# A 3x3 grouped convolution whose images are prepared ahead: parts made one image further ahead, from image 15 on

## The chip, the cores and the metric

The kernel runs on one core of one Trainium2 chip. The metric is the device time of one execution in microseconds (us); the figure given is the median of several runs.

## The reference

The input `x` is 160 images of 128 channels and 32 x 32 pixels in fp32. They are normalised, convolved with weights that are first brought onto a coarse grid, and added to the input:

```python
def _gn(v, G=32, eps=1e-5):            # groups of 4 channels, each image by itself
    g = v.reshape(B_, G, C_ // G, H_, W_)
    m = jnp.mean(g, axis=(2, 3, 4), keepdims=True)
    s = jnp.var(g, axis=(2, 3, 4), keepdims=True)
    return ((g - m) / jnp.sqrt(s + eps)).reshape(v.shape)

# weights: U is (5, 128*128*9); two levels of flooring over the range of U
s1 = (max(U) - min(U)) / 3;  v1 = s1 * floor(U / s1)
s2 = s1 / 5;                 v2 = s2 * floor((U - v1) / s2)
w = (v1 + v2).reshape(640, 128, 3, 3)

# image i uses weight set i % 5 (five groups of a grouped convolution), 3x3, padding 1
x = x + conv(_gn(x), w)
```

## The kernel before, in words

**Order of the images.** The kernel takes the images set by set: 32 images with the first weight set, then 32 with the second, and so on; "image i" below is a place in that order. A chunk is two images, 1 MB, loaded by one DMA. `xpool` holds `CHUNKS` of them.

**The arithmetic.** TensorE multiplies fp16 numbers, so a normalised image is split into a high and a low fp16 part and both are convolved. Output rows are made in pairs, an even and an odd one, from combinations of input rows (or, for a "combined" image, of input columns) and of weights, which takes fewer matmuls than nine taps for each. There are two kinds of image. A *direct* one (`combined(i)` false) gives `hi` (ScalarE, L645) and a low part: `lo` (VectorE, L748) and its row combinations `rows` (L761, L769, L770). A *combined* one gives `v` in fp32, made by GpSimd (L675, L705) and VectorE (`combine`: L687, L694), then `vh` on ScalarE (L735) and `vl` on VectorE (L741). Up to image 29 combined and direct images alternate; up to 129 three of five are combined; from 130 on three of four.

**TensorE's part.** `conv(i)` first runs `sums_of_pairs(i + 1)`: the sums and differences that both output rows of image i + 1 share, into two PSUM tiles `m2` and `m1` (`m1a`, `m1b`), which need `vl` or `rows` of image i + 1. Then `main(i)` adds the rest to the two banks `eo` of image i. Between the two, ScalarE copies `m2` out (`leave`, L888), and VectorE makes the start of both banks from `m1` and that copy (`pairs`, L900 for the even one and L902 for the odd one). When `conv(i)` is over, ScalarE copies the banks out (L926), and GpSimd issues a DMA that adds them to the output in HBM (L950), where the input has been stored from the chunk before (L965). The first three and the last four images are added by hand on VectorE instead (`by_hand`).

**Step i of the loop in `run`.** One step is one image on TensorE. The program is written in the order in which each engine's queue shall run it; nothing is reordered later. In step i (from image 3 on), before the change:

- VectorE: the low part or `vl` of image i + 2; one or two small instructions of the next weight set (`later.take`); `pairs(i + 1)`; the scales of a finished statistics group; `combine(i + 4)`.
- ScalarE: the first statistics pass of the images due (L241), the copy-out of image i - 1, `leave(i + 1)`, `hi` or `vh` of image i + 3, the second statistics pass (L248).
- GpSimd: the power of a statistics group (L286, then `scales_by_vector` with L307 and L309 on VectorE), then its part of `v` or of z for image i + 4 (L675 and L705, or L711). `beside_pairs` makes these wait for the last VectorE instruction but one of the low part, so that they run while VectorE is busy with PSUM in `pairs`. GpSimd and its DMA issue follow in the same queue.
- SP: loads a chunk when the images `CHUNKS` places before it have been read (`consumed`), and stores a chunk four steps after its load.

**Statistics.** Images are measured in groups of 2, 4 or 8, by ScalarE, eight of them by VectorE (`BY_VECTOR`); `ahead` says up to which image in step i. A group's numbers take three more steps over TensorE (L256, L273), `deviations_by_vector` (L296 to L302), ScalarE and GpSimd. `shift` (L309) is used only by `normalise`, on ScalarE, for the first image of a group when that is a direct one.

Of the kernel before, what the change touches and what calls it, by code (L numbers as in the profile page):

```python
# [11 lines left out]
ALU = mybir.AluOpType  # L12
# [9 lines left out]
NB = 2  # L22
# [14 lines left out]
class Later:  # L37


    def __init__(self, steps=(), pace=0.0):  # L40
        self.steps = iter(steps)
        self.pace, self.due = pace, 0.0
        self.scalar = False
# [131 lines left out]
def last_of(steps, last=None):  # L175
    for last in steps:
        pass
    return last
# [27 lines left out]
class Statistics:  # L206
# [5 lines left out]
    def __init__(self, nc, small, gavg, mhalf, nb, scale, name):  # L212
        self.nc, self.small, self.gavg, self.mhalf = nc, small, gavg, mhalf
        self.nb, self.scale, self.name = nb, scale, name
        self.late = False

        self.mv = self.tile("mv", [nb, 2])

# [85 lines left out]
    def scales_by_vector(self):  # L304

        vector = self.nc.vector
        vector.tensor_scalar_mul(self.rstd, self.rstd, self.scale)  # L307
        self.shift = self.tile("shift", [self.nb])
        vector.tensor_tensor(self.shift, self.ngm, self.rstd, ALU.mult)  # L309

    def scales(self):
        nc = self.nc
# [72 lines left out]
class Main:  # L385
# [21 lines left out]

    STAT_LEAD = 14  # L410
    LOAD_LEAD = 18
    CHUNKS = 12
    STEADY = 7
    BY_VECTOR = (8, 10, 11, 14, 19, 24, 29, 34)
    FIFTHS = 30
# [10 lines left out]
    def __init__(self, tc, ctx, keep, x, u, out):  # L426
        self.tc = tc
        nc = self.nc = tc.nc
        self.imgs, C, self.H, self.W = x.shape
        P = self.P = nc.NUM_PARTITIONS  # L430
        assert C == P and self.H * self.W == 1024
        self.per_set = self.imgs // N_SETS
        self.xv = x.rearrange("(b n) c h w -> n c b (h w)", n=N_SETS)
        self.ov = out.rearrange("(b n) c h w -> n c b (h w)", n=N_SETS)
        self.uv = u.rearrange("n (o i k) -> n o i k", o=C, k=TAPS)

        def pool(name, bufs, **kw):
            return ctx.enter_context(tc.tile_pool(name=name, bufs=bufs, **kw))

        self.const = pool("const", 1)  # L440
        self.qpool = pool("quant", 1)
        self.wpool = pool("weights", 2)
        self.upool = pool("u", 1)
        self.xpool = pool("x", self.CHUNKS)
        self.zpool = pool("z", 2)
        self.parts = pool("parts", 4)
        self.rows = pool("rows", 4)
        self.wide = pool("wide", 2)
        self.wide_parts = pool("wide_parts", 3)
        self.evac = pool("evac", 2)  # L450
        self.sums = pool("sums", 3)
        self.unread = pool("unread", 1)
        self.small = pool("small", 3)
        self.ps_eo = pool("ps_eo", 2, space=PSUM)
        ps_m = pool("ps_m", 1, space=PSUM)
        ps_small = pool("ps_small", 1, space=PSUM)
        self.steps = Steps(nc, keep)

        self.m1a, self.m1b, self.m2_ps = (
            ps_m.tile([P, self.H // 2, self.W], F32, tag=name, name=name)  # L460
            for name in ("m1a", "m1b", "m2")
        )
        self.pair = [self.m1a, self.m2_ps]

        small = ps_small.tile([P, 512], F32, tag="small", name="small")
        self.pt, self.pg = small[:, : ROW * P].rearrange("p (k o) -> p k o", k=ROW), small[:, ROW * P :]
        self.chunks, self.z, self.hi, self.v, self.eo, self.m2 = {}, {}, {}, {}, {}, {}
        self.sum, self.stored = {}, {}
        self.tables, self.wts, self.across = {}, {}, {}
        self.columns = []  # L470

        cuts = [0, 2, 4, 8, 12, 16, 20, *range(24, self.imgs + 1, 8)]
        self.groups = [range(a, b) for a, b in zip(cuts, cuts[1:])]
        self.group_of = {i: k for k, g in enumerate(self.groups) for i in g}
        self.stats = {}
# [131 lines left out]
    def stats_of(self, k):  # L607
        if k not in self.stats:
            self.stats[k] = Statistics(
                self.nc, self.small, self.gavg, self.mhalf, len(self.groups[k]),  # L610
                self.steps.lift, k,
            )
            self.stats[k].late = self.groups[k].start not in self.HURRIED
        return self.stats[k]

    def measure(self, i, stages=(0, 1)):
# [343 lines left out]
    def store_input(self, c):  # L960
# [6 lines left out]
            return  # L967
        self.stored.update((i, self.store(i)) for i in images)

    def consumed(self, c):  # L970

        return max(i + 2 if self.by_hand(i) else i - 2 for i in range(c * NB, c * NB + NB))

    def run(self):
        nc, P = self.nc, self.P
# [53 lines left out]
        def measure(stage, *images):  # L1029
            for i in images:  # L1030
                self.measure(i, (stage,))
# [73 lines left out]
        later, turned = Later(), []  # L1105
        for i in range(self.imgs):
# [30 lines left out]
            else:  # L1137
                j = i - 1
                self.conv(i, on_the_way)
            ahead = i + min(10 + i // 4, self.STAT_LEAD + 1)  # L1140
            to_measure = range(measured, min(self.imgs, ahead))
            measured += len(to_measure)
            if i == 2:
# [3 lines left out]
            if n + 1 < N_SETS:  # L1147
                if b == (4 if n == 0 else 1):
                    later = Later(
                        (s for col in self.COLS for s in self.make_column(n + 1, col, "later")),  # L1150
                        36 / (self.per_set - 6 - b),
                    )
# [4 lines left out]
            if i < self.FIRST:  # L1157

                if i == 0:
                    measure(0, 8, 9, 10)  # L1160
                if i == 1:
                    self.normalise(4)
                    self.high_part(4)
                if i == 2:
                    self.leave(3)
                    self.normalise(5)
                    measure(1, 9)
                    self.high_part(5)
                    self.pairs(3)
                    self.low_part(4)  # L1170
                    run(self.combinations(4))
                    measure(0, 11)
                self.residual(j)
            else:

                last = None
                if self.combined(i + 2):
                    last = last_of(self.low_combined(i + 2))
                elif i + 2 < self.imgs:
                    self.low_part(i + 2)  # L1180
                    later.take(1)
                    last = last_of(self.combinations(i + 2))
                last = later.take(2 if self.combined(i + 2) else 1, last)
                if i + 4 < self.imgs:
                    before = self.last_but_one(last)
                    for st in scaled:
                        self.after(st.power(), before)
                    self.beside_pairs(i + 4, before)
                if i > self.FIRST and self.by_hand(j):
                    self.residual(j)  # L1190
                for k in by_scalar:
                    self.measure(k, (0,))
                if i > self.FIRST and not self.by_hand(j):
                    self.residual(j)
                    self.accumulate(j)
                part = i + 3 < self.imgs and not self.combined(i + 3)
                if i + 1 < self.imgs:
                    self.leave(i + 1)
                for st in ready:
                    if not st.late:  # L1200
                        st.deviations()
                if part:
                    if self.by_scalar_too(i + 3):
                        self.normalise(i + 3)
                    self.high_part(i + 3)
                if self.combined(i + 3):
                    self.high_combined(i + 3)
                for k in by_scalar:
                    self.measure(k, (1,))
            for st in middle:  # L1210
# [7 lines left out]
            for n_of, col in turned:  # L1218
                self.keep_taps(n_of, col)
                if col == self.COLS[-1]:  # L1220
                    later = Later(self.sums_of_set(n_of), 3.0)
            turned = []

            if i >= self.FIRST:

                if i + 1 < self.imgs:
                    self.pairs(i + 1)
                for st in scaled:
                    st.scales_by_vector()
                if self.combined(i + 4):  # L1230
                    self.combine(i + 4)
                else:
                    later.take(1)
                later.take_scalar()
                if b in (self.per_set - 4, self.per_set - 2):
                    later.finish()
                for st in ready:
                    if st.late:
                        st.deviations_by_vector()
# [7 lines left out]
            while loaded * NB < self.imgs and (  # L1247
                loaded * NB < i + self.LOAD_LEAD if loaded < self.CHUNKS
                else i >= self.consumed(loaded - self.CHUNKS)
            ):  # L1250
# [54 lines left out]
```

## Time and profile before

| | |
|---|---|
| median of 3 runs | 968.95 us (968.45 to 969.02) |
| the profiled execution's own time | 968.17 us |
| its span in the profile | 966.4 us |
| granted TensorE clock | 0.998 |
| TensorE busy (matmuls) | 926.9 us, 96% |
| VectorE busy | 910.1 us, 94% |
| ScalarE busy | 862.0 us, 89% |
| GpSimd busy | 463.6 us, 48% |
| DMA | 254.22 MB, mean 263 GB/s |

Busy times of engines overlap, so they don't add up to the span. A TensorE that is full on average can still be stopped in single places, so the table says little by itself; which wait ends last is read place by place. In the lines of the profile, PE is TensorE, PEld its weight load, DVE VectorE, ACT ScalarE, POOL GpSimd and SP SyncE; L741 is line 741 of the kernel, and the names are the program's, without buffer numbers (so `m<-` is `m2`).

### The profile page before, as it was taken

How to read it: one execution, taken by the hardware profiler on the slowest of the kernel's cores; microseconds unless marked ns; L12 is line 12 of the kernel's file. 1: busy time of each engine (PE TensorE's matmuls, PEld its weight loads, DVE VectorE, ACT ScalarE, POOL GpSimd, SP SyncE). 2: the span in 40 equal slices, each digit the busy share in tenths (PEclk: the TensorE clock that was granted, in tenths of full speed). 3: DMA queues.
4: the chain of work that ended last, by engine and by line, in shares of the span. 5: the costliest groups of instructions: out<-in, count | busy, mean ns of one | idle time of the engine just before them, and what ended most of it. 6: DMA issues, size and time to landing. Idle time of an engine off the chain costs nothing.

```text
span 966.4 us, 13055 instructions
## 1 busy us (share of the span) xinstructions
PE 926.9 (96%) x4432; PEld 433.6 (45%) x4432; DVE 910.1 (94%) x1280; ACT 862.0 (89%) x1167; POOL 463.6 (48%) x477
## 2 busy tenths in 40 slices
PE   2999999999999999999999999999999999999997
PEld 1444444444444444444444444444444444444443
DVE  7999999999999999989999999999999998998995
ACT  5879999999999999999989999999989999998561
POOL 4345344446445444554355435534445545666550
PEclk9999999999999999999999999999999999999999
DMA  9079999999999999999999999999999999666663
GB/s 363 20 273 340 338 328 321 334 322 315 327 320 328 314 327 323 311 315 258 283 243 287 276 305 286 278 251 301 278 274 260 286 275 255 98 90 107 91 107 112
DMA packets 67450, 254.22 MB, mean 263 GB/s; under 512 B 5296, under 2 KB 5296, under 8 KB 67376
## 3 DMA queue, kind: packets, MB, share of 16 engines
q1 hardware_dynamic: 45344, 173.09, 47.6%
q0 software_dynamic: 22032, 80.23, 44.7%
q8 instruction: 36, 0.59, 0.2%
q14 instruction: 38, 0.31, 0.1%
HBM read 89.19 MB, written 164.10 MB: 262 GB/s over the span
## 4 chain that ended last, share of the span: by engine, by line


## 5 line engine op out<-in xcount | busy, mean ns | idle before, releaser
L785 PE MATMUL eo<-hi,wt 128*128 128x496 f16 (+3 forms) x1170 | 310.3, 375 | 0.9 <-ACT wt L567 0.9
L840 PEld LDWEIGHTS <-wt 128*128 128x128 f16 x1884 | 183.9, 99 | 211.5 <-DVE rows L770 1.7
L741 DVE SCALAR_TENSOR_TENSOR vl<-v,rstd,vh 128x2048 f16<-128x2048 f32 x94 | 221.5, 2356 | 1.0 <-ACT vh L735 0.9
L840 PE MATMUL eo<-vh,wt 128*128 128x512 f16 x561 | 210.2, 375 | 0.2 <-DVE eo L902 0.2
L840 PE MATMUL eo<-vl,wt 128*128 128x512 f16 x561 | 210.1, 375 | 0.0
L735 ACT ACTIVATE vh<-v,rstd 128x2048 f16<-128x2048 f32 x94 | 188.1, 2001 | 13.4 <-DVE v L694 13.0
L926 ACT COPY sum<-eo 128x1024 f32<-128x1024 f32 x153 | 160.7, 1050 | 29.4 <-PE eo L840 28.5
L675 POOL TENSOR_SCALAR v<-xt,ngm 128x64 f32<-128x64 f32 x94 | 83.0, 883 | 215.5 <-issue 66.8
L785 PEld LDWEIGHTS <-wt 128*128 128x128 f16 x1242 | 120.9, 99 | 140.2 <-DVE eo L902 2.6
L248 ACT ACTIVATE junk<-xt,mv 128x1024 uint8<-128x1024 f32 x152 | 174.4, 1147 | 0.1
L840 PEld LDWEIGHTS <-across 128*128 128x128 f16 x1128 | 110.3, 98 | 140.3 <-issue 13.3
L241 ACT ACTIVATE junk<-xt 128x1024 uint8<-128x1024 f32 x152 | 160.5, 1056 | 13.8 <-DMA xt<-in_x_dram 10.7
L711 POOL TENSOR_SCALAR z<-xt,ngm,rstd 128x1024 f32<-128x1024 f32 x49 | 90.5, 1847 | 155.9 <-DVE rows L769 45.9
L840 PE MATMUL eo<-rows,wt 128*128 128x512 f16 x378 | 143.5, 380 | 0.0
L950 POOL DMA_DIRECT2D out_dram<-sum x153 | 133.8, 876 | 9.5 <-ACT sum L926 6.1
L840 PE MATMUL m<-vl,across 128*128 128x496 f16 (+1 forms) x282 | 105.6, 374 | 9.5 <-DVE vl L741 9.5
L687 DVE TENSOR_TENSOR v<-xt 128x960 f32<-128x960 f32 x94 | 109.0, 1160 | 0.0
L840 PE MATMUL m<-vh,across 128*128 128x496 f16 (+1 forms) x282 | 105.6, 375 | 0.9 <-ACT m L888 0.9
L888 ACT ACTIVATE m<-m 128x512 f32<-128x512 f32 x157 | 93.8, 597 | 13.4 <-PE m L840 13.2
L705 POOL TENSOR_TENSOR v<-xt 128x512 f32<-128x512 f32 x94 | 97.2, 1034 | 0.0
L748 DVE TENSOR_TENSOR lo<-z,hi 128x1024 f16<-128x1024 f32 x66 | 80.6, 1220 | 0.0
L286 POOL TENSOR_TENSOR rstd<-ve,mhalf 128x8 f32<-128x8 f32 (+2 forms) x24 | 39.1, 1629 | 68.8 <-DVE rows L769 22.0
(150 smaller groups left out, 1182.3 us busy)
## 6 DMA issues: line engine op xcount, KB each, us to landing
xt<-in_x_dram SPq DMA_DIRECT2D x78, 1024.0 KB, 12.7
out_dram<-sum POOLq DMA_DIRECT2D x153, 512.0 KB, 8.8
out_dram<-xt SPq DMA_DIRECT2D x76, 1024.0 KB, 18.6
out_dram<-xt SPq DMA_DIRECT2D x7, 512.0 KB, 3.7
u<-in_L_conv_U_dram SPq DMA_DIRECT2D x4, 576.0 KB, 19.0
xt<-in_x_dram SPq DMA_DIRECT2D x4, 512.0 KB, 9.7
range<-in_L_conv_U_dram SPq DMA_DIRECT2D x3, 576.0 KB, 7.9
u<-in_L_conv_U_dram SPq DMA_DIRECT2D x2, 288.0 KB, 3.2
```

What stands on the lines that cost most here:

```text
L241: self.nc.scalar.activation(junk, image, ACTF.Copy, scale=-1.0 / image.shape[1], accum_out=self.mv[:, j, 0:1],)
L248: self.nc.scalar.activation(junk, image, ACTF.Square, bias=self.mv[:, j, 0:1], accum_out=self.mv[:, j, 1:2],)
L687: nc.vector.tensor_tensor(self.view(v, 1, (511, 2), (half, H), (1, half - 1)), self.view(x, 1, (1, 2), (W, H), (2, half - 1)), self.view(x ...
L705: ins = nc.gpsimd.tensor_sub(self.v[i][:, 1536:], odd, even)
L711: ins = nc.gpsimd.tensor_scalar(z, self.image(i), st.ngm[:, j], st.rstd[:, j], ALU.add, ALU.mult)
L735: self.nc.scalar.mul(vh, self.v[i], st.rstd[:, j])
L741: yield self.nc.vector.scalar_tensor_tensor(vl, self.v[i], st.rstd[:, j], self.hi[i], ALU.mult, ALU.subtract)
L785: nc.tensor.matmul(self.bank(target, a)[:, first:end, c0:c1], self.wts[n, col][:, k, :], tile[:, s0 : s0 + 2 * (end - first) - 1 : 2, c0 + ...
L840: self.nc.tensor.matmul(out, weights, moving, start=start and j == 0, stop=False, skip_group_check=True)
L888: self.nc.scalar.mul(m2, self.m2_ps, 0.5)
L926: nc.scalar.copy(self.as_banks(i, self.sum[i]), self.flat(i, eo))
L950: added = self.nc.gpsimd.dma_start(self.ov[n, :, b], self.sum.pop(i), accum_op=ALU.add)
```

## The change

Five things are changed together.

- From image 15 or 16 on, every part of an image is made one step earlier. `step_of(i, ahead)` gives the images whose parts belong to step i: `i + ahead` up to a certain step, two images in the one step where the lead grows (11 for `v`, 12 for `vh` and `hi`, 13 for the low part), and `i + ahead + 1` after it.
- The pools follow: `rows` has five buffers instead of four, `wide_parts` (for `vh`) four instead of three. `xpool` has eleven chunks instead of twelve, and `consumed` lets a chunk go one step earlier.
- Images are measured further ahead: `i // 3` instead of `i // 4` in the beginning, and up to 16 images ahead instead of 15.
- The small weight instructions are taken at slightly different places: one after `vl` instead of up to two, and one after `combine` in every step.
- `scales_by_vector` makes `shift` only for groups whose first image is direct: L309 runs eight times instead of nineteen.

The number of matmuls stays the same, and so does what is computed. The core of the diff:

```diff
+        if self.shifted:
+            self.shift = self.tile("shift", [self.nb])
+            vector.tensor_tensor(self.shift, self.ngm, self.rstd, ALU.mult)
...
-    STAT_LEAD = 14
+    STAT_LEAD = 15
+    FURTHER = 11
-    CHUNKS = 12
+    CHUNKS = 11
...
-        self.rows = pool("rows", 4)
+        self.rows = pool("rows", 5)
-        self.wide_parts = pool("wide_parts", 3)
+        self.wide_parts = pool("wide_parts", 4)
...
+            self.stats[k].shifted = not self.combined(self.groups[k].start)
...
+    def step_of(self, i, ahead):
+        change = self.FURTHER + 4 - ahead
+        return [k for k in range(i + ahead + (i > change), i + ahead + 1 + (i >= change)) if k < self.imgs]
...
-        return max(i + 2 if self.by_hand(i) else i - 2 for i in ...)
+        return max(i + 2 if self.by_hand(i) else i - 2 - (i > self.FURTHER + 6) for i in ...)
...
-            ahead = i + min(10 + i // 4, self.STAT_LEAD + 1)
+            ahead = i + min(10 + i // 3, self.STAT_LEAD + 1)
...
-                if self.combined(i + 2):
-                    last = last_of(self.low_combined(i + 2))
-                elif i + 2 < self.imgs:
-                    self.low_part(i + 2)
-                    later.take(1)
-                    last = last_of(self.combinations(i + 2))
-                last = later.take(2 if self.combined(i + 2) else 1, last)
-                if i + 4 < self.imgs:
+                for k in self.step_of(i, 2):
+                    if self.combined(k):
+                        last = last_of(self.low_combined(k), last)
+                    else:
+                        self.low_part(k)
+                        later.take(1)
+                        last = last_of(self.combinations(k), last)
+                last = later.take(1, last)
+                if last:
                     before = self.last_but_one(last)
                     for st in scaled:
                         self.after(st.power(), before)
-                    self.beside_pairs(i + 4, before)
+                    for k in self.step_of(i, 4):
+                        self.beside_pairs(k, before)
...
-                if part:
-                    if self.by_scalar_too(i + 3):
-                        self.normalise(i + 3)
-                    self.high_part(i + 3)
-                if self.combined(i + 3):
-                    self.high_combined(i + 3)
+                for k in self.step_of(i, 3):
+                    if self.combined(k):
+                        self.high_combined(k)
+                        continue
+                    if self.by_scalar_too(k):
+                        self.normalise(k)
+                    self.high_part(k)
...
-                if self.combined(i + 4):
-                    self.combine(i + 4)
-                else:
+                for k in self.step_of(i, 4):
+                    if self.combined(k):
+                        self.combine(k)
                     later.take(1)
```

More of the change, by code (lines that the diff above doesn't have):

```diff
@@ L214, in __init__ @@
         self.nb, self.scale, self.name = nb, scale, name
-        self.late = False
+        self.late = self.shifted = False
         self.mv = self.tile("mv", [nb, 2])
@@ L307, in scales_by_vector @@
         vector.tensor_scalar_mul(self.rstd, self.rstd, self.scale)
-        self.shift = self.tile("shift", [self.nb])
-        vector.tensor_tensor(self.shift, self.ngm, self.rstd, ALU.mult)
+        if self.shifted:
+            self.shift = self.tile("shift", [self.nb])
+            vector.tensor_tensor(self.shift, self.ngm, self.rstd, ALU.mult)
     def scales(self):
@@ L968, in store_input @@
         self.stored.update((i, self.store(i)) for i in images)
+    def step_of(self, i, ahead):
+        change = self.FURTHER + 4 - ahead
+        return [k for k in range(i + ahead + (i > change), i + ahead + 1 + (i >= change)) if k < self.imgs]
     def consumed(self, c):
-        return max(i + 2 if self.by_hand(i) else i - 2 for i in range(c * NB, c * NB + NB))
+        return max(i + 2 if self.by_hand(i) else i - 2 - (i > self.FURTHER + 6) for i in range(c * NB, c * NB + NB))
     def run(self):
@@ L1195, in run @@
                     self.accumulate(j)
-                part = i + 3 < self.imgs and not self.combined(i + 3)
                 if i + 1 < self.imgs:
```

## The prediction

> **What bounds the kernel now.** I read the page first, then the waits, then the stretches and the timeline. The page's busy line and its slices say who is full:
>
> ```profile
> PE 926.9 (96%) x4432; PEld 433.6 (45%) x4432; DVE 910.1 (94%) x1280; ACT 862.0 (89%) x1167; POOL 463.6 (48%) x477
> ...
> PE   2999999999999999999999999999999999999997
> ...
> DVE  7999999999999999989999999999999998998995
> ACT  5879999999999999999989999999989999998561
> ...
> DMA  9079999999999999999999999999999999666663
> ```
>
> TensorE is full from the third slice on, VectorE and ScalarE nearly so, and the DMA engines until slice 33. The waits of TensorE from 120 us to the end:
>
> ```profile
> PE m L840 <- DVE vl L741: 9.5, 9, 1.9
> PE m L840 <- ACT m L888: 0.9, 1, 0.9
> ```
>
> Columns: total us, times, longest. Matmul ends are modelled, so I also compared the starts of each image's convolution in the timeline with the shortest step of its kind: 3.83, 5.07 or 7.64 us (0.14 more with a statistics matmul). TensorE loses, by image:
>
> ```
> image         14    15    18    24(ACT) 63    73    78    118   134,142,150  others
> us lost       0.93  0.33  1.44  1.11    0.25  0.83  2.14  2.13  1.13 each    0.10     sum 12.65
> pairs' spare  0.0   0.0   0.5   -       0.97  0.70  0.0   0.0   0.97 each
> ```
>
> That is all the change can win in the loop: 12.65 us, 1.3%. The last row needs two timelines, TensorE and then VectorE around image 78:
>
> ```profile
> 494.51 0.38 PE L840 MATMUL m<-vh,across 128*128 128x512 f16 x1
> 496.83 0.38 PE L840 MATMUL m<-vl,across 128*128 128x512 f16 x1 [1.94 <-DVE vl L741]
> ...
> 499.24 0.59 PE L785 MATMUL eo<-hi,wt 128*128 128x512 f16 x2
> ```
>
> ```profile
> 494.44 2.34 DVE L741 SCALAR_TENSOR_TENSOR vl<-v,rstd,vh 128x2048 f16<-128x2048 f32 x1
> ...
> 497.75 0.69 DVE L900 SCALAR_TENSOR_TENSOR eo<-m1a,m 128x512 f32<-128x512 f32 x1
> 498.48 0.70 DVE L902 SCALAR_TENSOR_TENSOR eo<-m1a,m 128x512 f32<-128x512 f32 x1
> ```
>
> L741 ends at 496.78 and releases the matmul. But the first matmul on `eo` starts 0.06 us after L902 ends (499.18): the pairs were late too. "Spare" is the distance from L902's end to that matmul, less 0.09 which is always there. Where it is 0, an earlier `vl` alone would only move the wait to L902.
>
> The stretches show where VectorE has no idle time to give:
>
> ```profile
> 80.00:100.00 20.00, 20.00 (x98) 9.55 (x97) 19.69 (x36) 19.34 (x30) 6.95 (x8) 1.00 1.04 330
> 120.00:140.00 20.00, 19.24 (x93) 8.80 (x91) 19.73 (x34) 18.80 (x30) 8.51 (x8) 1.00 1.04 336
> ...
> 600.00:700.00 100.00, 100.00 (x479) 46.39 (x478) 97.59 (x132) 96.30 (x132) 46.05 (x47) 1.00 1.00 275
> ```
>
> Columns: length, then busy us (count) of PE, PEld, DVE, ACT, POOL, then clock, DMA share, GB/s. Around images 6 to 23 (72 to 182 us) VectorE runs without a gap; later it has 2 to 3% spare.
>
> [...]the trace has 2356 ns for L741, 2.26 us start to start. [...]L309 on 8 elements takes 0.17 us, but 0.97 us beside GpSimd's L705:
>
> ```profile
> 491.42 0.36 DVE L307 TENSOR_SCALAR rstd<-rstd,lift 128x8 f32<-128x8 f32 x1 [0.22 <-POOL rstd L286]
> 491.82 0.97 DVE L309 TENSOR_TENSOR shift<-ngm,rstd 128x8 f32<-128x8 f32 x1
> 492.70 1.15 DVE L687 TENSOR_TENSOR v<-xt 128x960 f32<-128x960 f32 x1
> ```
>
> [...]the early slices show 315 to 340.
>
> **The change, part by part.** VectorE prices are start to start in the timeline: `combine` (L687, L694) 1.73; `vl` 2.26; a direct image's four (L748, L761, L769, L770) 2.41; a pair 1.33; the five of `deviations_by_vector` 0.5.
>
> 1. *The lead (steps 11 to 13).* Nothing is added in total, but one image's parts come early. Laying both VectorE orders side by side, before the pairs of image 14 the changed one has done `combine` of 17, the low part of 16 and one set of deviations more: 1.73 + 2.41 + 0.5 = 4.6 us. Before those of 18 it is 1.73 + 2.41 = 4.1 us. VectorE has no gap there, so all of it is late. Delay of TensorE against a stall-free run: at 14, 4.6 + 0.93 - 0.0 = 5.5; at 18, 4.1 (extra work) + 2.70 (stalls up to there) - 0.5 (spare) = 6.3; at 22, 5.7; at 26, 5.4. The maximum counts: 6.3.
> 2. *Statistics earlier (`i // 3`, lead 15).* At step 6, image 18's sum and most of image 17's pass come before `leave(8)`: 2.3 us on ScalarE. `leave(8)` ended 1.06 us before VectorE's pairs of 8 began, so VectorE gets a gap of 1.25 us in its full stretch, and keeps it: 6.3 + 1.25 = 7.6. If ScalarE catches up it is nothing. At step 12 ScalarE has z and hi of 16 besides (2.3 us); that makes `leave(14)` end near 127.5 us, before VectorE comes to those pairs. The stall at 24 (ScalarE late by 1.1) goes: TensorE is by then later by more than ScalarE's extra work less its idle (6.8 us, mostly waits for `v`, between 105 and 175 us).
> 3. *Later stalls.* Removed: 12.65 - 3.81 (up to 24) = 8.84 us, if the pairs keep up too. Repricing their work: in the five-image pattern the pairs are needed 3.8, 5.1, 6.4, 5.1, 7.6 us apart; the largest excess of VectorE's work over it was 5.47 - 3.83 = 1.6 us (combine and low part meeting the short gap), and becomes 5.47 - 5.1 = 0.4. At 78: between the pairs of 75 and 78 VectorE took 21.3 us and will have 19.2 (one combine and 1.25 us of waiting fall elsewhere), which covers 2.14. At 118 the order is the same. From 130 on the excess adds up to 3.9 us in the step with statistics, of 5.9 us that VectorE is ahead when it last waited for TensorE. I leave 0.5 us for what the small weight steps do.
> 4. *`shift` for fewer groups.* Eleven L309 go. At 0.96 each that would be 5 us, but behind L309 stands L687, [...]which then waits for the same L705. I take 0.08 each, hidden; the other end is 0.9 each, all before pairs that no longer bind: nothing either.
> 5. *Buffers.* vh four and rows five for one more image in flight: no new wait, each slot is freed by a convolution that ScalarE's copy L926 has already waited for. `v` keeps two: combine of k and `vl` of k - 2 stay in one step. GpSimd's L675, L705, L711 and L286 move with their image, so they meet the same VectorE instructions; its L950 stays.
> 6. *Eleven chunks.* Each load is issued one step later on SP and first read one step earlier, about 11.5 us less cover. Late loads have 55 us. In the full DMA stretch a load lands 22 to 33 us after issue: chunk 23 landed at 217.2, read at 233.9. In the new SP order chunk c stands where c + 1 stood, with 1 MB less ahead (3.1 us at 336 GB/s): chunk 25 lands at 250.7 - 3.1 = 247.6, is read at 256.2 - 5.8 + 3.8 = 254.2. The least cover is 6.6 us: cost nothing.
>
> Sum: 7.6 + 0.5 - 12.65 = -4.5. The profiled execution took 968.17 (span 966.4), 0.8 under the median, so 963.7 for such a one and **964.4** for the median of 968.95.
>
> **The rivals.** *The wait changes its name* (0.17): `vl` is early but the pairs stay where they were, since VectorE's later work isn't rearranged as I think. Then a stall saves only its spare: 0.25 + 0.70 + 3 x 0.97 + 0.1 = 4.0 of the later 8.84, against 3.8 paid at the lead: 968.95 + 3.8 - 4.0 = 968.8. For it: spare 0 at 78 and 118. Against: item 3's work between pairs. *The loads come late* (0.13, slower): in the full stretch the cover of 6.6 us is gone, ScalarE's L241 waits for chunks 22 to 26, and what it waits TensorE loses. It decides when landings slip by more than 6.6 + 6.5 = 13 us against my reckoning, as much as the spread of 22 to 33 us and a step of SP queueing make; at 14 us, 968.95 - 4.5 + 7.4 = 971.9. Against: one chunk less in flight shortens the queue. *The lead is cheaper* (0.1): ScalarE absorbs item 2 and the deviations overlap: 6.0 instead of 7.6, 962.8. That the change doesn't do what it says is out: the orders show image 16's parts a step early and all later ones with it.
>
> **How the numbers follow.** The forecast has 0.6. Its own range is 962 to 967, from a lead of 5.5 to 9 us and residual stalls of 0 to 1.5. The 8-in-10 range reaches to the first rival and stops short of the second: 961.5 to 969.5. A measurement of this kernel tells 0.2%, 1.9 us, from no change: faster means under 967.0, slower over 970.9. Faster: 0.6 + 0.1 = 0.70; same 0.17; slower 0.13.
>
> **What would show it.** Right: no wait of TensorE for L741 after 180 us, steps of 77, 78, 117, 134, 142, 150 at 7.64 to 7.8 us, and 6 to 8 us lost between images 13 and 18, as waits for L902 or L741. VectorE's gap before the pairs of 8 shows item 2. Wrong: waits for L902 of 1 to 2 us at 78 and 118 (first rival); L241 waiting for xt at 220 to 270 us (second); a lead of over 10 us.

## The result, and the profile after

| | before | after |
|---|---|---|
| median, 11 runs each on one chip | 969.02 us (968.34 to 969.48) | 966.56 us (964.56 to 967.46) |
| ratio | | 0.9974, 95% interval 0.9966 to 0.9981 |
| profiled execution, its span | 968.17, 966.4 us | 964.56, 962.5 us |

The change gains 2.5 us, 0.26%; 4.5 were forecast. The profiled execution of the changed kernel is the fastest of its eleven, 2.0 us under their median. So the experiments begin with a second profiled execution of the same kernel, called *again* below (965.95 us, near its median). One of *again*'s nine runs, of 1412 us at a mean granted clock of 0.66, is slow and left aside.

Most lines of the kernel have moved by two or three: L741 (`vl`) is now L744, L900 and L902 (pairs) L903 and L905, L888 (`leave`) L891, L687 (`combine`) L690, L785 and L840 (matmuls) L788 and L843, L309 (`shift`) L310. Busy line and slices of the changed kernel:

```profile
PE 927.8 (96%) x4432; PEld 433.8 (45%) x4432; DVE 902.6 (94%) x1269; ACT 862.7 (90%) x1167; POOL 460.1 (48%) x477
...
PE   2899989999999999999999999999999999999997
...
DVE  7989999999899999989999999899999998999993
ACT  5879989999899999999999999999999999997660
...
DMA  9079999999999999999999999999999999856563
```

TensorE has a new digit 8 in the sixth slice (120 to 144 us), where the lead is paid, and one in the second, which is the start (last section). VectorE is 7.5 us less busy, with eleven instructions fewer. The waits of TensorE from 120 to 960 us (total us, times, longest):

```profile
PE m L843 <- DVE vl L744: 2.1, 1, 2.1
PE eo L788 <- DVE eo L905: 1.7, 2, 1.0
PE eo L843 <- DVE eo L905: 1.2, 3, 0.5
PE m L843 <- ACT m L891: 0.2, 1, 0.2
```

Before, nine waits for `vl` stood here. The one that is left, 2.1 us, is at image 14, in the lead. All later ones are gone, but three waits of L843 for pairs (L905), at images 37, 77 and 117, are new. The one at image 77 is shown in two timelines, of TensorE and then of VectorE:

```profile
494.31 0.81 PE L843 MATMUL m1a<-rows,wt 128*128 128x512 f16 x3
495.60 0.39 PE L843 MATMUL eo<-vh,wt 128*128 128x512 f16 x1 [0.47 <-DVE eo L905]
...
498.14 0.38 PE L843 MATMUL m<-vh,across 128*128 128x512 f16 x1
498.36 0.38 PE L843 MATMUL m<-vl,across 128*128 128x512 f16 x1
```

```profile
488.29 1.99 DVE L690 TENSOR_TENSOR v<-xt 128x960 f32<-128x960 f32 x1
...
491.39 2.34 DVE L744 SCALAR_TENSOR_TENSOR vl<-v,rstd,vh 128x2048 f16<-128x2048 f32 x1
...
494.84 0.70 DVE L905 SCALAR_TENSOR_TENSOR eo<-m1b,m 128x512 f32<-128x512 f32 x1
...
495.71 2.35 DVE L744 SCALAR_TENSOR_TENSOR vl<-v,rstd,vh 128x2048 f16<-128x2048 f32 x1
```

The matmul on `m` that needed `vl` and waited 1.94 us before (at 496.83) now follows its neighbour after 0.22 us (498.36): the `vl` made at 491.39 is a step old by then. In exchange, the pairs of 77 end at 495.54 and hold the matmul of 495.60.

The table gives the time in us between the starts of two images' convolutions, read from the timelines ("of it lost" is lost time from 3 to 20). A run without any stall from 3 to 20 would take 99.87 us: the 102.57 of before less its stalls at 14, 15 and 18.

```
profile of    image 3 starts   3 to 20   of it lost   20 to 158   3 to 158
before        60.59            102.57    2.70         785.75      888.32
after         61.72            106.41    6.54         777.30      883.71
again         60.49            108.47    8.60         777.33      885.80
```

From image 20 on, the gain is the same in both profiles, 8.4 us. From 3 to 20 the changed kernel loses 3.8 us more than the kernel before in one profile, and 5.9 in the other.

### The profile page after: what moved, and what is told of

It reads as the page before. It is cut to its first block, busy times and chain, and to the rows that moved or that the text cites. A ratio compares the mean times of both kernels' runs of the same rounds, so it can differ in the third digit from the quotient of the medians.

```text
span 962.5 us, 13034 instructions
## 1 busy us (share of the span) xinstructions
PE 927.8 (96%) x4432; PEld 433.8 (45%) x4432; DVE 902.6 (94%) x1269; ACT 862.7 (90%) x1167; POOL 460.1 (48%) x477
## 4 chain that ended last, share of the span: by engine, by line
## 5 line engine op out<-in xcount | busy, mean ns | idle before, releaser
L788 PE MATMUL eo<-hi,wt 128*128 128x496 f16 (+3 forms) x1170 | 310.8, 376 | 2.4 <-DVE eo L905 1.7
L843 PEld LDWEIGHTS <-wt 128*128 128x128 f16 x1884 | 183.9, 99 | 211.5 <-DVE eo L905 2.7
L744 DVE SCALAR_TENSOR_TENSOR vl<-v,rstd,vh 128x2048 f16<-128x2048 f32 x94 | 221.8, 2360 | 0.2 <-ACT vh L738 0.2
L843 PE MATMUL eo<-vh,wt 128*128 128x512 f16 x561 | 210.1, 375 | 1.2 <-DVE eo L905 1.2
L843 PE MATMUL eo<-vl,wt 128*128 128x512 f16 x561 | 210.1, 374 | 0.0
L788 PEld LDWEIGHTS <-wt 128*128 128x128 f16 x1242 | 121.2, 99 | 142.8 <-DVE eo L905 4.9
L678 POOL TENSOR_SCALAR v<-xt,ngm 128x64 f32<-128x64 f32 x94 | 79.1, 842 | 202.0 <-DVE vl L744 86.9
L241 ACT ACTIVATE junk<-xt 128x1024 uint8<-128x1024 f32 x152 | 160.5, 1056 | 13.3 <-DMA xt<-in_x_dram 10.0
L714 POOL TENSOR_SCALAR z<-xt,ngm,rstd 128x1024 f32<-128x1024 f32 x49 | 93.3, 1904 | 165.1 <-DVE rows L773 55.0
L843 PEld LDWEIGHTS <-across 128*128 128x128 f16 x1128 | 110.8, 98 | 131.9 <-issue 4.9
L843 PE MATMUL eo<-rows,wt 128*128 128x512 f16 x378 | 143.5, 380 | 0.0
L690 DVE TENSOR_TENSOR v<-xt 128x960 f32<-128x960 f32 x94 | 114.0, 1212 | 0.0
L843 PE MATMUL m<-vl,across 128*128 128x496 f16 (+1 forms) x282 | 106.4, 377 | 2.1 <-DVE vl L744 2.1
L891 ACT ACTIVATE m<-m 128x512 f32<-128x512 f32 x157 | 93.7, 597 | 14.1 <-PE m L843 13.7
L843 PE MATMUL m<-vh,across 128*128 128x496 f16 (+1 forms) x282 | 106.2, 376 | 0.2 <-ACT m L891 0.2
L708 POOL TENSOR_TENSOR v<-xt 128x512 f32<-128x512 f32 x94 | 97.2, 1034 | 0.0
L286 POOL TENSOR_TENSOR rstd<-ve,mhalf 128x8 f32<-128x8 f32 (+2 forms) x24 | 42.3, 1761 | 65.1 <-DVE rows L773 21.1
```

The lines of the kernel that those rows point to most:

```text
L241: self.nc.scalar.activation(junk, image, ACTF.Copy, scale=-1.0 / image.shape[1], accum_out=self.mv[:, j, 0:1],)
L690: nc.vector.tensor_tensor(self.view(v, 1, (511, 2), (half, H), (1, half - 1)), self.view(x, 1, (1, 2), (W, H), (2, half - 1)), self.view(x ...
L708: ins = nc.gpsimd.tensor_sub(self.v[i][:, 1536:], odd, even)
L714: ins = nc.gpsimd.tensor_scalar(z, self.image(i), st.ngm[:, j], st.rstd[:, j], ALU.add, ALU.mult)
L744: yield self.nc.vector.scalar_tensor_tensor(vl, self.v[i], st.rstd[:, j], self.hi[i], ALU.mult, ALU.subtract)
L788: nc.tensor.matmul(self.bank(target, a)[:, first:end, c0:c1], self.wts[n, col][:, k, :], tile[:, s0 : s0 + 2 * (end - first) - 1 : 2, c0 + ...
```

## The experiments

The theory: the forecast's parts are right, and two of its terms are too small, VectorE's gap before the pairs of 8 (item 2) and the stalls that remain later (item 3). Its rivals: the loads come late after all, the lead costs what it costs wherever it is put, and the later gain is due to fewer `shift`. Ratios are to the kernel before on the same chip. All edits but that of *b_ring11* are made to the changed kernel.

**again**: no edit.

> The changed kernel once more, unchanged. In the loop (start of image 3's convolution to that of image 158's) the first profile is 4.6 us shorter than before, by my reckoning -4.5, but the medians differ by only 2.5 us. Theory A (the start is what varies): the loop is again 840 +- 0.5 us long (883.7 from conv(3) to conv(158) in the first profile), and what a typical execution takes more than the first profile's 964.56 us lies ahead of image 3 (it starts at 61.7 us there) or behind the last. Theory B (late loads): the loop itself is 1 to 2 us longer in a typical execution, with ScalarE's first statistics pass waiting for a chunk. Time 966.0 to 967.0 either way.

Measured: 966.32 us (median of eight runs from 965.46 to 967.43), ratio 0.9975 (0.9965 to 0.9986). The loop is 2.1 us longer than in *after*, so the start alone (the first expectation) is not what varies. VectorE in the timeline, first in *after*, then in *again*:

```profile
90.06 0.70 DVE L903 SCALAR_TENSOR_TENSOR eo<-m1a,m 128x512 f32<-128x512 f32 x1 [0.16 <-ACT m L891]
```

```profile
90.92 0.70 DVE L903 SCALAR_TENSOR_TENSOR eo<-m1a,m 128x512 f32<-128x512 f32 x1 [2.30 <-ACT m L891]
```

The gap that item 2 put at 1.25 us is 0.16 in one execution and 2.30 in the other. The difference, 2.14, is the difference of the two up to image 20 (108.47 - 106.41 = 2.06). In *after* VectorE was ready for these pairs 1.28 us later than in *again* (89.90 against 88.62), and `leave(8)` ended 0.86 us earlier (90.03 against 90.89). The second part is seen in ScalarE's waits from 60 to 92 us, again *after* and then *again*:

```profile
ACT nnn L134 <- DMA u<-in_L_conv_U_dram: 0.5, 1, 0.5
...
```

```profile
ACT nnn L134 <- DMA u<-in_L_conv_U_dram: 2.4, 1, 2.4
ACT junk L241 <- DMA xt<-in_x_dram: 0.9, 1, 0.9
```

ScalarE waits for a load of the next weights and, in *again*, for one of images. What it loses there stands ahead of `leave(8)`. In *after*, TensorE and VectorE came to images 3 to 8 about 1.2 us later (61.72 against 60.49), so the load held ScalarE for 0.5 us only. The two waits were 1.6 and 1.0 us before, without harm: `leave(8)` still had 1.06 us to spare. So a late start can hide the gap; what makes it longer than forecast is another thing, item 2 of the account below.

**b_ring11**: the kernel before, with one line of the change.

```diff
-    CHUNKS = 12
+    CHUNKS = 11
```

> The kernel before with eleven chunk places instead of twelve, nothing else. Theory A (the ring is free, as my prediction priced it): ratio 1.000 +- 0.001, image 3 starts at 60.6 +- 1.3 us, the loads of chunks 18 to 26 keep over 3 us of cover before their first reader. Theory B (the ring costs what the change didn't gain): 1.5 to 2.5 us slower, by waits of ScalarE for a chunk or by a later image 3.

Measured: 968.91 us, ratio 0.9999 (0.9991 to 1.0007); 888.31 us from image 3 to 158, against 888.32. The smaller ring costs nothing, and the rival of the late loads falls with it. In the changed kernel, where chunks are read a step earlier besides, L241 waits for no chunk between 200 and 280 us in either profile; the least time from landing to reading of chunks 12 to 25 was 14.0 us.

**vec24**: image 24 is measured by ScalarE.

```diff
-    BY_VECTOR = (8, 10, 11, 14, 19, 24, 29, 34)
+    BY_VECTOR = (8, 10, 11, 14, 19, 29, 34)
```

> The changed kernel with image 24 measured by ScalarE instead of VectorE: 1.6 us less for VectorE just ahead of the pairs of image 14, and 2.4 us more for ScalarE. Theory A (VectorE's work sets the lead's cost): the step of image 14 falls from 12.3 to about 10.7 us and the total by 1.0 to 1.6 us. Theory B (ScalarE is as late there: its copy of m2 for image 14 ended 0.05 us before it was needed): TensorE waits for L891 instead, step 13 grows by what step 14 loses, and the total is the same or up to 1 us more.

Measured: 965.88 us, ratio 0.9969 (0.9958 to 0.9979); 8.35 us lost from 3 to 20. Half a microsecond under *again* is inside the scatter. Step 14 falls from 13.18 to 10.36 us, but step 13 grows from 5.06 to 6.36. The waits from 62 to 165 us, of TensorE and then of VectorE:

```profile
PE eo L788 <- DVE eo L905: 3.3, 2, 2.3
PE m L843 <- ACT m L891: 1.6, 2, 1.1
PE small L273 <- DVE dv L302: 1.1, 1, 1.1
...
```

```profile
DVE eo L903 <- ACT m L891: 2.4, 1, 2.4
DVE twice L296 <- ACT wt L569: 0.6, 1, 0.6
```

The gap before the pairs of 8 is there as in *again*. The fall of step 14 is no measure of the edit: 2.9 us of that step are, in *again*, a stretch at half rate (last section) which this profile doesn't have. The sum is no clean measure either, since the profile is already late at image 8: step 7 takes 5.25 us against 4.49, with 1.1 of the 1.6 us of waits for L891, and ScalarE had waited 2.1 instead of 0.9 us for the load of an image at 61 us. *shiftall* below has the same wait and the same step 7 (5.28), and beside its 9.40 us *vec24* lost 1.05 less. Before the pairs of 14, VectorE is spared the measuring of image 24, 1.7 us, and 0.6 of it come back as a wait for ScalarE's copy of the next weights (L569). So VectorE's work is one cause of the lead's cost, and part of what leaves it comes up as ScalarE's.

**stat4** and **stat4b**: the early part of the statistics is undone, twice the same kernel.

```diff
-            ahead = i + min(10 + i // 3, self.STAT_LEAD + 1)
+            ahead = i + min(10 + i // (4 if i < 14 else 3), self.STAT_LEAD + 1)
```

> The changed kernel, measuring up to step 13 no further ahead than before (i // 4 instead of i // 3); from step 14 on as changed. Theory A (item 2 of the prediction, mis-sized: the earlier statistics pass makes ScalarE late with m2 of image 8, 2.3 us of VectorE's full stretch in a typical execution instead of 1.25): no gap of VectorE ahead of the pairs of 8, no extra 0.5 us in steps 7, 11 and 13, steps 12 to 18 lose 6 to 7 us instead of 8.7; 1.3 to 2.3 us under the changed kernel, ratio to before 0.9955 +- 0.0010. Theory B (the gap is taken up anyway, what is late is the extra image's work alone): the same time as the changed kernel within 0.5 us.

> stat4 unchanged, for a second profiled execution. Its first one showed a loop 1.0 us shorter than the typical one of the changed kernel, while the medians differ by 2.9. Theory A (after the pause at image 14 TensorE ran its matmuls 0.42 instead of 0.21 us apart for 2.1 us, which was 1.05 us lost and not covered, since no wait followed at image 18): median again 963.3 to 963.9, and a profile without that stretch has a loop of 883.3 to 883.9 and a wait of VectorE's making at image 18. Theory B (the 2.9 came of that chip or of the start): median 964.5 to 965.5.

Measured: 963.51 us, ratio 0.9951 (0.9938 to 0.9965), and 963.50, ratio 0.9944 (0.9930 to 0.9957). The gap before the pairs of 8 is at most 0.16 us in both. In *stat4b* 6.62 us are lost from 3 to 20, 2.0 less than in *again*; the loop takes 883.85 us, which is 4.5 less than before, as forecast for the change. The earlier statistics cost the change 2 to 3 us and brought nothing that shows here.

The first execution lost 7.62 us. The waits of TensorE from 120 to 165 us, of *stat4* and then of *stat4b*:

```profile
PE eo L788 <- DVE eo L905: 2.3, 1, 2.3
PE m L843 <- DVE vl L744: 2.0, 1, 2.0
...
```

```profile
PE m L843 <- DVE vl L744: 2.0, 1, 2.0
PE eo L788 <- DVE eo L905: 1.1, 2, 0.6
...
```

After these pauses TensorE ran some matmuls at half its rate in both, as the last section shows. In *stat4* that was from 134.0 to 137.4 us, after the pairs of 14, and no wait followed at 18. In *stat4b* it was from 129.1 to 132.6, ahead of these pairs, and the waits for VectorE at 14 (0.6 us) and in the step of 18 (0.7) took it in. So the expectation of a profile without such a stretch was wrong, while its loop time (883.3 to 883.9) was met; and the stretch in *stat4* cost 1.7 us, not the 1.05 that the expectation names. In these two profiles a half-rate stretch counts only where TensorE isn't held for VectorE afterwards.

**stat4v**: *stat4* with the edit of *vec24*.

> stat4 (963.5) with image 24 measured by ScalarE instead of VectorE. Theory A (VectorE's queue alone sets the lead at images 14 to 18): one pass of about 1.2 us leaves it, so 962.3, and image 14's step falls from 14.0 to about 12.8 us. Theory B (ScalarE is as close to the limit there: with the faster i // 3, the same edit moved half of the saving into waits for L891): the step of 14 shortens and step 12 or 13 grows by waits for L891; 963.0 to 963.6, not told apart from stat4.

Measured: 963.00 us, ratio 0.9938 (0.9924 to 0.9951). Lost from 3 to 20: 4.94 us, 1.7 less than in *stat4b*, but 0.7 come back at image 22. Of the two expectations the second holds: by the medians, the half microsecond isn't told apart from *stat4*.

**lead62** and **lead62m**: the lead is taken at image 66 instead of 15, statistics as before. In the first the sixteenth image ahead is measured from step 50, in the second from step 24.

```diff
-    FURTHER = 11
+    FURTHER = 62
...
-            ahead = i + min(10 + i // 3, self.STAT_LEAD + 1)
+            ahead = i + min(10 + i // 4, self.STAT_LEAD + (i >= self.FURTHER - 12))
```

> The change with its lead taken at images 64 to 67 (steps 62 to 64) instead of 15 to 18, the measuring going 16 ahead from step 50 on. Theory A (the lead costs what VectorE can't absorb): the stalls at 14, 15, 18 and 24 are back as before (3.8 us), but the lead at 64 meets VectorE's gaps of 0.95 and 1.27 us and spare pairs of 2 us, so it costs 0 to 1.5 us instead of the 6.6 measured at 13 to 18; later stalls stay away (about 1.3 us at 77 and 117). Loop sum about 1.5 us under the changed kernel: ratio to before 0.9955 to 0.9965. Theory B (the lead costs the same anywhere, as two images' parts in one step): 4 to 5 us at 64 to 66, and the time is 1.5 to 3 us above the changed kernel.

> The lead at images 64 to 67 as in the run before, but measuring grows to 16 ahead at step 24 by i // 4, not in step 50. Theory A: the 2.2 us that steps 52, 53 and 58 lost there (two images measured in one step ahead of them) are gone, the lead still costs about 2 us in 63 to 71, the stalls at 14, 15, 18 and 24 stay at 3.8 us: 1.5 to 2.5 us under the run before, ratio to before 0.9935 to 0.9950. Theory B (those stalls came from the shorter cover of the loads or the lead's steps): steps 52, 53 and 58 stay long, same time as before.

(*lead62m* has `self.STAT_LEAD + 1` in place of the last sum.)

Measured: 965.45 us, ratio 0.9962 (0.9950 to 0.9975), and 965.65, ratio 0.9968 (0.9956 to 0.9980). From 3 to 20 only 3.52 us are lost, but 20 to 158 takes 782.5 instead of 777.3. In the second, by step: 25 1.3, 53 1.4, 66 0.4, 71 1.5 us, and the stall at 24 stays (1.0). In the first, measuring two images in one step cost 0.7 at 52 and 0.55 at 58, which the second hasn't; 53 has another cause, which stays open. So the lead itself costs about 1.9 us there (63 to 71), near the first expectation for *lead62*, but the gain forecast for *lead62m* (a ratio of 0.9935 to 0.9950) didn't come, and by the medians both are 2 us slower than *stat4*, which has the same statistics up to step 13 and pays its lead at image 15.

**lead30m** and **lead30s**: the lead at image 34; measured further from step 24 or from step 28.

```diff
-    FURTHER = 11
+    FURTHER = 30
...
-            ahead = i + min(10 + i // 3, self.STAT_LEAD + 1)
+            ahead = i + min(10 + i // 4, self.STAT_LEAD + (i >= 28))
```

(*lead30m* has `self.STAT_LEAD + 1` there.)

> The same with the lead at images 32 to 35 (steps 30 to 32), where VectorE had gaps of 1.4 us and spare pairs of 2 to 5 us in the kernel before, and no weights are made. Theory A: 0 to 2 us lost in 31 to 38, and the 0.25 us at 63 saved too: within 0.7 us of the lead at 64. Theory B (the lead costs 5 us or more wherever the next 40 images are as full as these): 2 to 4 us above it.

> The lead at FURTHER 30 as in lead30m (964.4), with the sixteenth image ahead measured from step 28 instead of step 24, so that two images fall to ScalarE in step 28 and one in step 24. Theory A (step 25 of lead30m was 5.12 us because ScalarE measured two images in step 24): step 25 is 3.8 to 3.9, time 963.1, unless step 29 takes the same 1.3. Theory B (VectorE's queue made it): step 25 stays at 5.1 and the time at 964.4.

Measured: 964.41 us, ratio 0.9954 (0.9941 to 0.9968), and 963.17, ratio 0.9940 (0.9927 to 0.9954). Step 25 takes 5.12 us in the first and 3.83 in the second; step 29 doesn't take it over. The waits of TensorE from 200 to 270 us, *lead30m* and then *lead30s*:

```profile
...
PE m L843 <- ACT m L891: 1.0, 1, 1.0
...
```

```profile
PE eo L788 <- DVE eo L905: 0.9, 2, 0.5
PE eo L843 <- DVE eo L905: 0.5, 1, 0.5
```

The wait for ScalarE at 25 is gone, shown to come from the step in which two images are measured. The lead itself, steps 31 to 37, costs about 2 us here. But the stalls at images 14, 15, 18 and 24, which an early lead takes in, stay: 3.4 us in *lead30s*. So its loop, 882.56 us, is only 1.3 us shorter than that of *stat4b*, and the medians, 963.17 and 963.50, don't tell the two apart.

**lead30v**: *lead30s* with the edit of *vec24*.

> lead30s (963.17) with image 24 measured by ScalarE. Theory A (VectorE alone sets the stalls at images 14, 15 and 18 there, 0.5, 0.4 and 1.5 us): they shrink by up to 1.3 us, 961.9. Theory B (ScalarE has no room around image 24, where lead30s waits 0.9 us for L891): the wait there grows by what the others lose, 963.0 to 963.6.

Measured: 961.84 us (961.45 to 962.81), ratio 0.9930 (0.9917 to 0.9944), the lowest median of all; its interval overlaps that of *stat4v*, which has the same measuring and the early lead. Only 1.32 us are lost from 3 to 20, and the stall before image 24 (1.0 us) hasn't grown, so the first expectation holds. Its waits of TensorE from 120 to 960 us:

```profile
PE eo L843 <- DVE eo L905: 1.5, 3, 0.5
PE m L843 <- DVE vl L744: 1.1, 1, 1.1
PE m L843 <- ACT m L891: 0.9, 1, 0.9
PE eo L788 <- DVE eo L905: 0.8, 2, 0.4
```

**shiftall**: `shift` is made for all groups, as before.

```diff
-            self.stats[k].shifted = not self.combined(self.groups[k].start)
+            self.stats[k].shifted = True
```

> The changed kernel with shift (L309 before) made for all nineteen groups again. Theory A (item 4: without it the next instruction, L687, waits for the same GpSimd instruction, so that leaving it out saves 0.08 us each): the time is that of the changed kernel within 0.4 us; L687's mean falls from 1212 to about 1160 ns, and the shift instructions last 0.96 us where GpSimd's L705 runs beside. Theory B (it saves its whole length): up to 11 x 0.9 us more VectorE work; 1 to 2 us slower, as waits for the pairs at 77, 117, 133, 141, 149.

Measured: 966.60 us, ratio 0.9980 (0.9972 to 0.9987), against 966.56 and 966.32 for the changed kernel. From 20 to 158 it takes 777.62 us, 0.3 more; from 3 to 20 its profile lost 9.40, with the gap before the pairs of 8 at 2.36 us. That is 0.8 more than in *again*, and it stands in step 7 (5.28 against 4.49 us), as in *vec24*, after the same longer wait of ScalarE for an image at 61 us (2.1 against 0.9 us), so early that no extra `shift` is made yet. By the medians and the later part, the eleven instructions bring some 0.3 us at most. Where the time goes is seen when L310 is left out. VectorE in *shiftall*, then in *after*:

```profile
489.69 0.37 DVE L307 TENSOR_SCALAR rstd<-rstd,lift 128x8 f32<-128x8 f32 x1 [0.22 <-POOL rstd L286]
490.10 0.96 DVE L310 TENSOR_TENSOR shift<-ngm,rstd 128x8 f32<-128x8 f32 x1
490.98 1.15 DVE L690 TENSOR_TENSOR v<-xt 128x960 f32<-128x960 f32 x1
```

```profile
487.92 0.36 DVE L307 TENSOR_SCALAR rstd<-rstd,lift 128x8 f32<-128x8 f32 x1 [0.22 <-POOL rstd L286]
488.29 1.99 DVE L690 TENSOR_TENSOR v<-xt 128x960 f32<-128x960 f32 x1
```

L690 takes the waiting over, 1.99 instead of 1.15 us. Over all 94 of them that is 114.0 instead of 109.4 us. Six of the 94 last 1.99 us in *after*, each with GpSimd's L708 beside it for 0.96 or 0.97 us of that; the other 88 last 1.15 to 1.26 us, with L708 beside them for 0.24 at most. In the kernel before the same is seen at L309: nine of the nineteen last 0.96 or 0.97 us, each with L705 beside it for 0.93, and the ten without it last 0.16 or 0.17. So where a long one is left out, the next instruction can take the time over, 0.84 us in each of six places; why either is held is not shown.

## Why the prediction was right or wrong

In the loop it gave -4.5 us, and its sum can be set beside *again*, which of the two profiled executions is nearer the median: lead 8.60 instead of 7.6, and 20 to 158 8.4 gained instead of 9.45. Each is 1 us short, which makes -2.5. The median moved by 2.5 too. That the first profile met the forecast almost exactly (883.71 from 3 to 158, 4.6 less than before) is luck: its late start hid the gap of item 2.

1. *The lead: right.* 6.3 us were worked out from the extra work before the pairs of 18. Less VectorE's gap before the pairs of 8, the profiles lost 6.54 - 0.16 = 6.4 (*after*), 8.60 - 2.30 = 6.3 (*again*) and, with at most 0.16 of gap, 6.6 (*stat4b*). The maximum does stand at 18: the step of 18 is still 0.65 to 1.15 us too long in these three. *stat4* is the exception: its half-rate stretch, which the forecast didn't have, puts the maximum at 14, with 7.6 us.
2. *Earlier statistics: the right mechanism, mis-sized.* The gap is there and ends with `leave(8)`, but it is 2.30 us long in *again* and 2.36 in *vec24* and *shiftall*, where 1.25 was forecast. ScalarE's share was right: `leave(8)` ends at 90.89 in *again* and at 88.49 before, 2.4 us later, where 2.3 was forecast. The step that failed is "ended 1.06 us before VectorE's pairs of 8 began": this spare belongs to VectorE's old order. VectorE before, then in *again*:

```profile
88.42 0.35 DVE L146 TENSOR_TENSOR k<-nnn,lt 128x384 f16<-128x384 int16 x1
88.80 0.75 DVE L162 SCALAR_TENSOR_TENSOR rest<-k,s1n,u 128x384 f32<-128x384 f16 x1
89.47 0.69 DVE L900 SCALAR_TENSOR_TENSOR eo<-m1a,m 128x512 f32<-128x512 f32 x1
```

```profile
88.27 0.35 DVE L146 TENSOR_TENSOR k<-nnn,lt 128x384 f16<-128x384 int16 x1
90.92 0.70 DVE L903 SCALAR_TENSOR_TENSOR eo<-m1a,m 128x512 f32<-128x512 f32 x1 [2.30 <-ACT m L891]
...
94.00 0.73 DVE L162 SCALAR_TENSOR_TENSOR rest<-k,s1n,u 128x384 f32<-128x384 f16 x1
```

The weight instruction L162, 0.7 us start to start, stood ahead of these pairs. By the fourth part of the change it stands behind `combine`, so VectorE is ready that much sooner and waits that much longer; the forecast put nothing for the small weight steps here. Of the other 0.4 us, 0.1 are ScalarE's and 0.15 VectorE's, which has come that much sooner; the rest stays open. This is read from the order of the instructions; no run puts L162 back. Without the earlier statistics (*stat4*, *stat4b*) the spare is gone all the same, with gaps of at most 0.16 us, and the time is 963.5, under the forecast. The rest of the item was right: no gap of VectorE at 14, and the stall at 24 is gone (step 23: 4.94 to 3.83 us).
3. *Later stalls: right in what goes, mis-sized in what stays.* Steps 78, 118, 134, 142 and 150 are at 7.64 to 7.70 us, 73 at 7.78, 63 at 7.64. But steps 37, 77 and 117 are 0.45, 0.65 and 0.67 longer than before, 1.8 in all where 0.5 was left "for what the small weight steps do". All three are waits for L905. At 77 the working (21.3 us of VectorE, 19.2 after) held for 78 and was not done for the image before it: from L905 of 76 to L903 of 77 VectorE now takes 7.12 us, with the scales (L307), a `combine` whose L690 lasts 1.99 us, two weight instructions and a `vl`, where 5.75 us with the low part of a direct image stood before.
4. *`shift`: right*, within 0.3 us (*shiftall*).
5. *Buffers: right*; no wait for a buffer is to be seen. The parts were not tried one by one.
6. *Eleven chunks: right* (*b_ring11*). The least cover was 14.0 us (chunk 22), where the least worked out was 6.6 (chunk 25, which had 19.6: it landed 12 us earlier than reckoned).

*The wait changes its name* is refuted by 78 and 118: both stood at spare 0, and both are gone without a wait for L905. It is true in a small way at 77 and 117. *The loads come late* is refuted. *The lead is cheaper* did not come, but can be had: without the earlier statistics 6.6 us are lost from 3 to 20 instead of 8.6 (*stat4b*).

What was not foreseen at all is that the place of the lead was open. The forecast took VectorE's full stretch, images 6 to 23, as the place to pay in. At image 34 the same extra work cost 2 us; what this brings in the whole is less, because the stalls up to image 24 then stay.

## What to carry to other kernels

A lead of one item costs its extra work once, and costs it in full where the engine that makes it has no gap; put it where that engine has waits of its own, let the measuring that it needs grow in another step, and count the stalls that the old place would have taken in. A spare time that is read before a change holds only as long as both engines keep their order ahead of it: here one moved instruction of 0.7 us used up most of 1.06. And a profile with a late start can hide a wait that the others have. When a late part is brought forward, work out the engine's order for the items before and after the stall too, since its work is not less but elsewhere.

## What the runs showed of the hardware

**A pause of TensorE can cost more than its length.** *again*, TensorE in the timeline after the wait for `vl` at image 14, and the stretches there (length, busy us and count of PE, PEld, DVE, ACT, POOL, then granted clock, DMA share, GB/s):

```profile
130.70 0.58 PE L843 MATMUL m<-vl,across 128*128 128x512 f16 x1 [2.42 <-DVE vl L744]
131.08 0.62 PE L843 MATMUL m<-vh,across 128*128 128x496 f16 x1
131.50 0.62 PE L843 MATMUL m<-vl,across 128*128 128x496 f16 x1
...
136.61 0.38 PE L843 MATMUL eo<-rows,wt 128*128 128x512 f16 x1
136.82 0.80 PE L788 MATMUL eo<-hi,wt 128*128 128x496 f16 x3
```

```profile
126.00:130.00 4.00, 1.81 (x9) 0.73 (x8) 3.90 (x12) 4.00 (x6) 0.00 (x0) 0.96 1.05 361
130.00:134.00 4.00, 3.30 (x8) 1.13 (x8) 4.00 (x8) 3.56 (x7) 0.23 (x1) 0.50 1.02 341
134.00:138.00 4.00, 3.99 (x14) 1.41 (x13) 3.97 (x6) 2.81 (x4) 2.14 (x3) 0.69 1.02 418
```

Fourteen matmuls come 0.42 us apart instead of 0.21, and the clock falls to 0.50: 2.9 us on top of the wait of 2.4. It was 1.6 us in *after* and 1.7 in *stat4* and *stat4b*. The length of the pause doesn't decide it alone: such a stretch followed pauses of 1.97 us (*stat4b*), 2.08 (*after*), 2.42 (*again*) and 2.43 (*shiftall*), and a pause of 2.27 us was followed by one in *stat4* (5 us after another pause, of 1.98 us, that none had followed) and by none in *vec24*. What else decides it is not shown. Between 30 and 950 us the granted clock is 1.00 throughout in the profile of before. In that of *after* it is 1.00 but for two stretches at 0.50, of 3.4 us each (40.9 to 44.3 and 129.7 to 133.1); the windows above make it 6.8 us in *again*. In *after*, *again* and *stat4b* TensorE was held for VectorE at image 18 all the same, which takes the loss in; in *stat4* it wasn't, and the loop was 1.0 us longer than in its second profile.

**The start moves by 1.2 us between executions.** Image 3 starts at 60.4 to 60.9 us in most profiles, at 61.72 in *after*, 61.60 in *lead30s* and 61.49 in *b_ring11*. In these three, and in no other profile, a half-rate stretch of 3.4 us lies between 40 and 45 us, in which the matmuls take 1.7 us more; so the late start goes with this stretch. TensorE before, then in *b_ring11*:

```profile
39.95 1.44 PE L785 MATMUL eo<-hi,wt 128*128 128x496 f16 x6 [0.58 <-ACT wt L567]
```

```profile
39.93 2.40 PE L785 MATMUL eo<-hi,wt 128*128 128x496 f16 x6 [0.58 <-ACT wt L567]
```

All profiles also begin with matmuls 0.42 us apart instead of 0.21, up to 24 to 27 us, and that end doesn't go with the start of image 3: it is 23.9 us in *after* and in *again* alike.
